# A decoder block on Trainium2: layer-norm scalings of a closed pair taken together, and gates turned at another place

## The chip, the cores and the metric

One core of a Trainium2 chip runs the whole kernel in one launch. The metric is the device time in microseconds. The core has five engines with queues of their own: TensorE (PE in the profile, its weight loads PEld), VectorE (DVE), ScalarE (ACT), GpSimd (POOL) and SyncE (SP), which issues all the DMA transfers named here.

## The reference, cut to what matters

`x` is (16, 256, 512) in float32. Three layers follow each other, each with its own residual and layer norm: a state-space mixer, a long convolution with multiplicative heads, and a feed-forward layer with two of eight low-rank experts for each token.

```python
# second layer (v = x, both factors = ctx), eight heads to a group
kv = vr[:, :, :, None, :] * x2r[:, :, None, :, :]
y = irfft(rfft(kv, n=1024) * k_f[None, :, None, None, :], n=1024)[..., :512]
y = y + kv * skip
out = einsum('bhijl,bhil->bhjl', y, x1r)
...
# third layer
base = x_flat @ W.T + b
logits = x_flat @ gate_w.T + gate_b
topk_logits, topk_idx = top_k(logits, 2)
gates = softmax(topk_logits)
xA = einsum('nd,erd->ner', x_flat, lora_A)
out = base + sum over the two chosen experts of gate * (xA @ lora_B)
...
x = layernorm(x + mixer(x))
x = layernorm(x + long_convolution(x))
x = layernorm(x + feed_forward(x))
```

## The kernel before

The first half of the kernel (up to about 750 us) is the mixer; the change doesn't touch it. The second half is one Python loop over 32 heads (`for h in range(HX)`). The order in which instructions are written is the order in each engine's queue: the kernel asks for a manual schedule, so that nothing is reordered, and only the waits are derived.

A head is a tile of 128 tokens' rows by 512. In iteration `h` the kernel does the long convolution of head `h` and, beside it, the feed-forward layer of head `f = h - 1`.

The convolution is a product with blocks of a Toeplitz matrix. It runs twice in each head, for the halves `q = 0` and `q = 1` of the batch, and accumulates in the four PSUM banks of `y`. Each half begins with `seeded` (L1013), a matmul into the last bank; ScalarE then copies parts of it into another bank (`spread_seed`, L1020); then `convolve` runs the full blocks (L1031) and the triangular ones in quadrants (L1046). In the midst of the quadrants TensorE waits for a tiny ScalarE copy, `one` (L1062), which itself waits for the first quadrants. When a half is done, VectorE multiplies the two pairs of banks by the context (`multiplied`, L1079, tile `pr`) and sums them (`reduced`, L1089, tile `red`). `y` has one buffer for each pair of banks, so the next seed can only be written when the first of the two products has read its bank. VectorE also makes the next head's `kv` (L157, `products`).

At the start of an iteration TensorE transposes the next head's `v` (`turned_v`, L147, copied by ScalarE at L149). Then come matmuls of the feed-forward layer as filling, then the seed.

The feed-forward layer of head `f` goes in these steps. GpSimd adds `ol` (L1412), ScalarE squares it (L1191), GpSimd folds the squares (L1195). `products_with_gates`, behind the first convolution, transposes the folded squares (L1211), multiplies `ol` by the gates' and low-rank weights (L1213) into the PSUM tile `gl`, and also transposes the gated low-rank products `xa` of the head before (L1209) into free columns of the new `gl` (`XAT`, the last 128); ScalarE copies that to `xaT` (L1225). `spread_of` makes the layer norm's factor `rs_h` on GpSimd (L1235). `gates` is a chain of small VectorE operations with one exponential on ScalarE (L1128 to L1147), ending in `xa`.

The dense product is done for two heads together with seven half products instead of eight (`class Pair`): `first`, `second`, `third_and_fifth`, `fourth`, `sixth`, `seventh` (all L1271) into the PSUM tiles `al` and `be`, and the low-rank additions `lora_of_first` and `lora_of_second`. Sums of inputs (`S`, L1289) are made on GpSimd. A pair that starts with `f` odd takes `f` and `f + 1`; from the next even `h` it is `closing`. `common` makes the shared sums `u` and `m` on VectorE; `scaled_first` and `scaled_others` make scaled copies `ua`, `ub`, `mb` on GpSimd (L1328, L1329). Head 0 of the feed-forward layer goes alone (`base`, `alone`).

The last layer norm of a head is `finish`: two VectorE scalings with running sums into `x3` (L1161), a negative mean on GpSimd (`nm_c`, L1103), a square with a sum on ScalarE (L1112), and three small GpSimd operations (L1114, L1115, L1166). `store` is one ScalarE activation (`res`, L1171) and a DMA. Before the change, head 0 of a closing pair is finished behind the second convolution of an even `h` and stored at the start of the next iteration behind the seed; head 1 is finished in the first half of that odd `h` and stored in its second half.

The order in the odd iteration, before the change:

```python
                if ready is not None:
                    store(*ready)
...
                elif closing is not None:
                    ready = closing.finish(1, folded)
```

and at the end of the even one:

```python
                convolve(y, kv, T, Td, 1)
                if closing is not None:
                    ready = closing.finish(0, closing.scaled_others)
```

Behind the loop, the last head's second convolution runs with `late=True`: quadrants first, then six full blocks, with the remaining steps of the last pair put between them (`steps`: `second`, `turn`, `lora_of_first`, `first_finished`, `rest`). The last head's own feed-forward layer and three stores follow.

Of the kernel before, what the change touches and what calls it, by code (L numbers as in the profile page):

```python
# [8 lines left out]
F32 = mybir.dt.float32  # L9
AF = mybir.ActivationFunctionType  # L10
# [62 lines left out]
def decoder_kernel(  # L73
# [843 lines left out]
    with ExitStack() as s2:  # L917
# [180 lines left out]

        def centred_squares(src, total, tag, between=None):

            nm = p2.tile([P, 1], F32, tag=f"nm_{tag}", name=f"nm_{tag}")
            if total.shape[1] == 2:
                nc.gpsimd.tensor_scalar(  # L1103
                    nm, total[:, 0:1], total[:, 1:2], -1.0 / D, ALU.add, ALU.mult
                )
            else:
                nc.gpsimd.tensor_scalar(nm, total, -1.0 / D, None, ALU.mult)
            if between is not None:
                between()
            sq = p2.tile([P, D], F32, tag="sq", name="sq")  # L1110
            var = p2.tile([P, 1], F32, tag=f"var_{tag}", name=f"var_{tag}")
            nc.scalar.activation(sq, src, AF.Square, bias=nm, accum_out=var)  # L1112
            rs = p2.tile([P, 1], F32, tag=f"rs_{tag}", name=f"rs_{tag}")
            nc.gpsimd.tensor_scalar(var, var, 1.0 / D, LN_EPS, ALU.mult, ALU.add)  # L1114
            nc.gpsimd.tensor_tensor(rs, var, nhalf[:, 0:1], ALU.pow)  # L1115
            return nm, rs

        def gates(gl, rs, room=None):
# [37 lines left out]

        def finish(h, parts, rs, between=None):
            x3 = p2.tile([P, D], F32, tag="x3", name="x3")
            total = p2.tile([P, len(parts)], F32, tag=f"sum_c{len(parts)}", name="sum_c")
            for n, (cols, ps, own) in enumerate(parts):  # L1160
                nc.vector.scalar_tensor_tensor(  # L1161
                    x3[:, cols], ps, rs, own, ALU.mult, ALU.add, accum_out=total[:, n : n + 1]
                )
            nm, rs = centred_squares(x3, total, "c", between)
            nb = p2.tile([P, 1], F32, tag="nb", name="nb")
            nc.gpsimd.tensor_tensor(nb, nm, rs, ALU.mult)  # L1166
            return h, x3, nb, rs

        def store(h, x3, nb, rs):
            res = p2.tile([P, D], F32, tag="res", name="res")  # L1170
            nc.scalar.activation(res, x3, AF.Identity, bias=nb, scale=rs)  # L1171
            nc.sync.dma_start(out[h * P : (h + 1) * P, :], res)

# [30 lines left out]

        def products_with_gates(o_l, sq, xa):

            gl = ps_t.tile([P, D], F32, tag="tr", name="gl")
            if xa is not None:
                nc.tensor.transpose(gl[0:ER, XAT], xa.rearrange("p e r -> p (e r)"), ident)  # L1209
            turned = gl[:, NG + 2 : NG + 2 + P]  # L1210
            nc.tensor.transpose(turned, sq, ident)  # L1211
            for kc in range(KD):
                nc.tensor.matmul(  # L1213
                    gl[:, 0 : NG + 2], o_l[:, kc, :], w_gl[:, kc, :],
                    start=(kc == 0), stop=(kc == KD - 1), skip_group_check=True,
                )
            ms = p2.tile([P, 1], F32, tag="ms", name="ms")
            nc.scalar.activation(
                sq, turned, AF.Identity, bias=eps, scale=1.0 / D, accum_out=ms
            )  # L1220
            return gl, ms

        def turned_copy(room):
            xaT = p2.tile([ER, P], F32, tag="xaT", name="xaT")
            nc.scalar.copy(xaT, room[0:ER, 0:P])  # L1225
            return xaT

        def spread_of(gl, ms):
# [9 lines left out]
        def turned_gates(xa, room):  # L1238
            nc.tensor.transpose(room[0:ER, 0:P], xa.rearrange("p e r -> p (e r)"), ident)
            return turned_copy(room)  # L1240

# [34 lines left out]
        class Pair:  # L1276
# [86 lines left out]

            def finish(self, head, between=None):
                return finish(self.f + head, self.parts(head), self.rs[head], between)

        last, xa = None, None
        pair, closing, ready = None, None, None
        for h in range(HX):
# [9 lines left out]
            if h:  # L1379
                if nxt:  # L1380
                    v_after = turned_v(vns.pop(0), ps_t, "tr")
                    kvs.append(load_T(h + 1))
                    if h + 2 < HX:
                        vns.append(load_v(h + 2))
                        cTs.append(load_c(h + 2))
                opened = pair if pair is not None and len(pair.o) == 2 else None
                if h == 2:
                    feed_forward(base, alone, (1,))
                if h == 3:
                    lora(base, xaT, ALL)  # L1390
                if opened is not None:
                    opened.sixth()
                if closing is not None:
                    closing.seventh()
                seed = seeded(y, T, xs, 0, h == 1)
                spread_seed(y, seed, h == 1)
                if ready is not None:
                    store(*ready)
                    ready = None
                if h == 2:  # L1400
                    feed_forward(base, alone, (2,))
                if opened is not None:
                    opened.second()
                if closing is not None:
                    closing.lora_of_second()
            if h < 2:
                weight_differences((3, 1) if h == 0 else (2, 4))
            if ff:
                for i, pr in zip(order, prs):
                    reduced(pr, red_f, 1, i)  # L1410
                o_l = p2.tile([P, NL, P], F32, tag="ol", name="ol", bufs=3)
                nc.gpsimd.tensor_tensor(  # L1412
# [5 lines left out]
                sq, folded = squares(o_l)  # L1418
                if h == 3:
                    ready = finish(0, ((ALL, base, b_bc),), rs_alone, folded)  # L1420
                elif closing is not None:
                    ready = closing.finish(1, folded)
                    closing = None
                else:
                    folded()
                if pair is not None and len(pair.o) == 2:
# [8 lines left out]
            red = p2.tile([P, NQ, NL, BQ * NH], F32, tag="red", name="red")  # L1435
            convolve(y, kv, T, Td, 0, late=h == 0, ahead=None if h else ahead)
            if h == 0:
                v_after = vT_ahead[0]
# [20 lines left out]
            if ff:  # L1459
                gl, ms = products_with_gates(o_l, sq, xa)  # L1460
                if xa is not None:
                    xaT = turned_copy(gl[:, XAT])
                    for one in (pair, closing):
                        if one is not None and one.f <= f - 1 <= one.f + 1:
                            one.xaT.append(xaT)
                if second:
                    pair.first()
                if closing is not None:
                    closing.fourth()
                    closing.scaled_first()  # L1470
                rs = spread_of(gl, ms)
                if second and nxt:
                    pair.sums_second()
            if nxt:
                seed = seeded(y, T, xs, 1, h == 0)
            if ff:
# [14 lines left out]
                if closing is not None:  # L1491
                    closing.lora_of_first()
            if ready is not None:
                store(*ready)
                ready = None
            if nxt:
                spread_seed(y, seed, h == 0)
            if nxt:
                products(v_n, cT_n, kv_n, 1)
# [5 lines left out]
            if ff:  # L1505
                if second and nxt:
                    pair.sums_third()
                if not nxt:
                    pair.common()
                xa = gates(gl, rs, gl[:, NG + 2 :])  # L1510
            if nxt:
                convolve(y, kv, T, Td, 1)
                if closing is not None:
                    ready = closing.finish(0, closing.scaled_others)
            else:
                pair.scaled_first()
                pair.scaled_others()
# [4 lines left out]
        o_f, red_f, y_f, cT_f = last  # L1522
        gl_f, o_l = gl, {}

# [45 lines left out]

        def turn():
            pair.xaT.append(turned_gates(xa, gl_f[:, XAT]))
            pair.fourth()
# [5 lines left out]
        def first_finished():  # L1579
            ready.append(pair.finish(0))  # L1580

# [20 lines left out]
        nc.tensor.matmul(base, xaT, w_lb, start=False, stop=True, skip_group_check=True)  # L1602
        store(*ready[0])
        store(*pair.finish(1))
        x3 = p2.tile([P, D], F32, tag="x3", name="x3")
# [80 lines left out]
```

## Time and profile before

| what | value |
|---|---|
| median of 3 runs | 1414.12 us (1413.99 to 1414.58) |
| the profiled execution | 1413.62 us, span 1411.80 us |
| TensorE busy | 1396.9 us, 99% of the span, 7091 matmuls |
| VectorE busy | 1178.7 us, 83% |
| GpSimd busy | 612.9 us, 43% |
| ScalarE busy | 429.2 us, 30% |
| granted TensorE clock | 0.998 |
| VectorE waiting for the convolution (L1079 on L1046) | 56.5 us in 46 waits |

A profile is one execution. In a timeline line the columns are the start in us, the length in us, the engine, the line of the kernel, the operation, output and inputs, and shapes; `x4` says that four such instructions are merged, and brackets give the idle time of the engine ahead of it and what ended that. Ends of matmuls are modelled, so for TensorE the distance from one start to the next says more than a length.

### The profile page before, as it was taken

The numbers are of one execution on the slowest core, as the hardware profiler recorded it, in microseconds if no ns is written. First come the engines' busy times: TensorE is split into PE (matmuls) and PEld (weight loads), VectorE is DVE, ScalarE is ACT, GpSimd is POOL, SyncE is SP. The second block draws the span as 40 slices with busy tenths as digits, with TensorE's granted clock in tenths as the row PEclk, the third lists the DMA queues.
The fourth block names the chain that finished last, engine by engine and source line by source line (L and its number), as shares of the span: only waits on it lengthen the run. The fifth ranks groups of instructions, "written<-read, shape, count | busy, mean of one in ns | idle before, by whom it ended". The sixth has DMA issues, their size and how long they took to land.

```text
span 1411.8 us, 19609 instructions
## 1 busy us (share of the span) xinstructions
PE 1396.9 (99%) x7091; PEld 949.5 (67%) x7091; DVE 1178.7 (83%) x2269; ACT 429.2 (30%) x948; POOL 612.9 (43%) x818
## 2 busy tenths in 40 slices
PE   9999999999999999999999999999999999999997
PEld 7888888788888888878885445454545554555444
DVE  6988878878888787877857888888989888989886
ACT  2423323233232332332311223333323233333331
POOL 5450011110100201001005577788777777887774
PEclk9999999999999999999999999999999999999999
DMA  8113111120121111202103112221222122212200
GB/s 304 33 38 133 36 57 46 38 84 8 46 77 46 52 40 39 85 18 81 47 8 116 50 48 75 76 68 53 75 68 68 45 75 75 75 47 74 68 25 32
DMA packets 49170, 89.22 MB, mean 63 GB/s; under 512 B 8880, under 2 KB 13360, under 8 KB 49072
## 3 DMA queue, kind: packets, MB, share of 16 engines
q1 hardware_dynamic: 49072, 87.96, 19.1%
q8 instruction: 56, 0.92, 0.3%
q14 instruction: 42, 0.34, 0.1%
HBM read 70.62 MB, written 17.32 MB: 62 GB/s over the span
## 4 chain that ended last, share of the span: by engine, by line
PE 95%; DVE 2%; issue 1%; DMA 1%; POOL 0%; ACT 0%; SPq 0%; POOLq 0%; DVEq 0%; ACTq 0%
PE mm L330 21%; PE y L1031 15%; PE s L330 14%; PE y L1046 12%; PE s L782 6%; PE mm L782 6%; PE y L1013 4%; PE be L1271 4%; PE al L1271 3%; PE gl L1213 2%; PE tr L147 1%; PE xm L599 1%; PE mm L739 1%; PE mm L873 1%; PE al L1243 1%; PE s L873 1%
## 5 line engine op out<-in xcount | busy, mean ns | idle before, releaser
L1079 DVE TENSOR_TENSOR pr<-y,cT 128x1024 f32<-128x1024 f32 x126 | 148.3, 1219 | 56.5 <-PE y L1046 56.5
L1046 PE MATMUL y<-kv 64*64 64x512 f32 x1536 | 179.8, 598 | 1.5 <-ACT one L1062 1.5
L588 DVE SCALAR_TENSOR_TENSOR acc<-xi,wc,acc 128x512 f32<-128x512 f32 x192 | 141.9, 753 | 7.4 <-ACT acc L584 1.7
L1089 DVE TENSOR_REDUCE red<-pr 128x128 f32<-128x1024 f32 x126 | 147.1, 1209 | 0.0
L157 DVE TENSOR_TENSOR kv<-tr,cT 128x1024 f32<-128x1024 f32 x124 | 145.4, 1214 | 0.0
L1046 PEld LDWEIGHTS y<-kv 64*64 64x64 f32 x1536 | 52.2, 132 | 120.3 <-issue 96.4
L1031 PE MATMUL y<-kv 128*128 128x512 f32 x272 | 128.5, 594 | 1.9 <-DVE pr L1079 1.7
L68 POOL TENSOR_TENSOR rs_a<-ve_a,nhalf 128x1 f32<-128x1 f32 x32 | 18.9, 592 | 242.7 <-DVE ve_a L66 242.7
L391 POOL TENSOR_TENSOR rstd<-ms,nhalf 128x4 f32<-128x4 f32 (+1 forms) x9 | 8.5, 949 | 251.6 <-DVE ms L389 251.6
L1031 PE MATMUL y<-kv,Td 128*128 128x512 f32 x248 | 116.6, 592 | 0.0
L330 PE MATMUL mm<-XT,w_z 128*128 128x256 f32 x384 | 90.7, 379 | 0.0
L1031 PEld LDWEIGHTS y<-kv,Td 128*128 128x128 f32 x248 | 47.2, 190 | 59.2 <-issue 55.6
L1020 ACT COPY y<-y 64x512 f32<-64x512 f32 x120 | 67.0, 558 | 45.4 <-PE y L1013 43.1
L997 POOL TENSOR_TENSOR xs<-kv 128x512 f32<-128x512 f32 x63 | 80.2, 1273 | 0.1
L1031 PEld LDWEIGHTS y<-kv 128*128 128x128 f32 x272 | 51.1, 190 | 42.7 <-ACT y L1020 17.9
L330 PEld LDWEIGHTS mm<-XT,w_z 128*128 128x128 f32 x384 | 73.1, 190 | 9.7
L330 PE MATMUL mm<-xnT,w_z 128*128 128x256 f32 x288 | 70.8, 382 | 0.0
L1412 POOL TENSOR_TENSOR ol<-o,red 128x512 f32<-128x512 f32 x31 | 39.3, 1269 | 68.3 <-DVE red L1089 68.3
L223 POOL TENSOR_TENSOR XT<-xnT 128x512 f32<-128x512 f32 x7 | 9.3, 1335 | 129.0 <-PE mm L782 123.7
L1013 PE MATMUL y<-xs,kv 128*128 128x512 f32 x120 | 63.8, 613 | 0.6
L330 PE MATMUL s<-XT,w_xi 128*128 128x256 f32 x256 | 61.0, 380 | 0.7 <-DVE XT L226 0.5
L330 PEld LDWEIGHTS mm<-xnT,w_z 128*128 128x128 f32 x288 | 54.1, 190 | 10.0 <-issue 3.0
(335 smaller groups left out, 3058.0 us busy)
## 6 DMA issues: line engine op xcount, KB each, us to landing
cT<-in_ctxT SPq DMA_DIRECT2D x32, 384.0 KB
kv<-in_toep SPq DMA_DIRECT2D x32, 384.0 KB
xt<-in_x SPq DMA_DIRECT2D x32, 256.0 KB
spread<-both SPq DMA_DIRECT2D x32, 256.0 KB
first<-xt SPq DMA_DIRECT2D x32, 256.0 KB
vn<-first SPq DMA_DIRECT2D x32, 256.0 KB
out<-res SPq DMA_DIRECT2D x31, 256.0 KB
xnT<-in_xT SPq DMA_DIRECT2D x7, 1024.0 KB
```

Source lines behind the costliest of these rows:

```text
L157: last = nc.vector.tensor_tensor(kv[:, q, k * BQ : (k + NL // 2) * BQ], vT[:, q, blks].rearrange("p k (b i) -> p (k b) i", i=NH).unsqueeze ...
L330: nc.tensor.matmul(ps, w[:, p, a, kc, :], Xs[b][:, kc, :], start=start and kc == 0, stop=stop and kc == 1, skip_group_check=upon,)
L588: ins = nc.vector.scalar_tensor_tensor(acc, xi[:, :, k : k + S], wc[:, c, k : k + 1], acc, ALU.mult, ALU.add)
L782: nc.tensor.matmul(ps, own[a][c][:, n * P : (n + 1) * P], w_o[b][c], start=start and c == 0, stop=stop and c == HC - 1, skip_group_check=upon,
L997: return nc.gpsimd.tensor_tensor(xs[:, q], moving(kv, q, 0), moving(kv, q, 1), ALU.add)
L1013: nc.tensor.matmul(seed, T[:, SHARED_AT, :], xs[:, q], start=True, stop=True)
L1020: nc.scalar.copy(bank_of(y, 2)[b : b + HP], seed[a : a + HP])
L1031: nc.tensor.matmul(bank_of(y, lb), w, moving(kv, q, mb), start=not late and lb not in begun, stop=False, skip_group_check=True,)
L1046: return nc.tensor.matmul(bank_of(y, lb)[cols], T[rows, DIAGONAL_AT, (b - a) * HP : (b - a + 1) * HP], moving(kv, q, lb)[rows], start=star ...
L1079: nc.vector.tensor_tensor(pr.rearrange("p (k b j) i -> p k b j i", k=2, j=NH), y[i].rearrange("p k (b j i) -> p k b j i", j=NH, i=NH), cT[ ...
L1089: nc.vector.tensor_reduce(red[:, q, 2 * i : 2 * i + 2, :].rearrange("p k t -> p (k t)"), pr, AX.X, ALU.add)
L1271: nc.tensor.matmul(ps, a[:, kc, :], w[:, kc, :], start=(start and kc == 0), stop=(kc == 1), skip_group_check=True,)
```

## The change

It has four parts.

- `finish` and `store` become a class `Finish`, so that its steps can be placed one by one: the constructor has the two VectorE scalings, then `mean`, `squares`, `spread`, and `store`; `whole` does the three in the middle at once.
- Both heads of a closed pair are scaled together in the first half of the odd iteration, behind the last sums (`reduced`) of the convolution of the head before. The means of both follow `ol` on GpSimd; the square and the factors of head 0 stand around the folding; those of head 1 behind the first convolution. Both are stored behind the second seed's copies. `scaled_others` moves ahead of the second convolution of the even iteration.
- The transpose of `xa` leaves `products_with_gates`. It now stands at the start of the next iteration, behind the transposes of `v`, and goes into the old `gl`.
- The gates of the pair's last head leave the loop and are made in `turn`, inside the last convolution; so ScalarE's exponential stands behind `one` in its queue. `pair.common` moves to the same branch as the last `scaled_first` and `scaled_others`.

The operations and their shapes stay the same; places change, and each GpSimd mean of a single sum reads one column of a two-column tile.

```diff
-        def finish(h, parts, rs, between=None):
...
+        class Finish:
+            def __init__(self, h, parts, rs):
...
+                for n, (cols, ps, own) in enumerate(parts):
+                    nc.vector.scalar_tensor_tensor(
+                        self.x3[:, cols], ps, rs, own, ALU.mult, ALU.add,
+                        accum_out=self.total[:, n : n + 1],
+                    )
...
-        def products_with_gates(o_l, sq, xa):
+        def products_with_gates(o_l, sq):
             gl = ps_t.tile([P, D], F32, tag="tr", name="gl")
-            if xa is not None:
-                nc.tensor.transpose(gl[0:ER, XAT], xa.rearrange("p e r -> p (e r)"), ident)
...
+                if xa is not None:
+                    xaT = turned_gates(xa, gl[:, XAT])
+                    if h == 2:
+                        xaT_alone = xaT
+                    else:
+                        pair.xaT.append(xaT)
...
                 spread_seed(y, seed, h == 1)
-                if ready is not None:
-                    store(*ready)
-                    ready = None
...
                 for i, pr in zip(order, prs):
                     reduced(pr, red_f, 1, i)
+                ready = []
+                if h == 3:
+                    ready = [Finish(0, ((ALL, base, b_bc),), rs_alone)]
+                elif closing is not None:
+                    ready = [closing.finish(head) for head in range(2)]
+                    closing = None
...
                 sq, folded = squares(o_l)
-                if h == 3:
-                    ready = finish(0, ((ALL, base, b_bc),), rs_alone, folded)
-                elif closing is not None:
-                    ready = closing.finish(1, folded)
-                    closing = None
-                else:
-                    folded()
+                for one in ready:
+                    one.mean()
+                for one in ready[:1]:
+                    one.squares()
+                folded()
+                for one in ready[:1]:
+                    one.spread()
...
             convolve(y, kv, T, Td, 0, late=h == 0, ahead=None if h else ahead)
+            for one in ready[1:]:
+                one.squares()
+                one.spread()
...
-                gl, ms = products_with_gates(o_l, sq, xa)
-                if xa is not None:
-                    xaT = turned_copy(gl[:, XAT])
...
+                gl, ms = products_with_gates(o_l, sq)
...
-            if ready is not None:
-                store(*ready)
-                ready = None
             if nxt:
                 spread_seed(y, seed, h == 0)
+            for one in ready:
+                one.store()
...
-                if not nxt:
-                    pair.common()
-                xa = gates(gl, rs, gl[:, NG + 2 :])
+                if closing is not None:
+                    closing.scaled_others()
+                if nxt:
+                    xa = gates(gl, rs, gl[:, NG + 2 :])
             if nxt:
                 convolve(y, kv, T, Td, 1)
-                if closing is not None:
-                    ready = closing.finish(0, closing.scaled_others)
             else:
+                pair.common()
                 pair.scaled_first()
                 pair.scaled_others()
...
         def turn():
+            xa = gates(gl_f, rs_f, gl_f[:, NG + 2 :])
             pair.xaT.append(turned_gates(xa, gl_f[:, XAT]))
...
-        store(*ready[0])
-        store(*pair.finish(1))
+        ready[0].store()
+        pair.finish(1).whole().store()
```

More of the change, by code (lines that the diff above doesn't have):

```diff
@@ L1097, in contract @@
                 reduced(pr, red, q, i)
[L1099 to L1105, printed above, removed]
-            else:
[L1107 to L1116, printed above, removed]
         def gates(gl, rs, room=None):
@@ L1155, in gates @@
             return xa
-        def finish(h, parts, rs, between=None):
[L1158 to L1172, printed above, removed]
+        class Finish:
+            def __init__(self, h, parts, rs):
+                self.h = h
+                self.x3 = p2.tile([P, D], F32, tag="x3", name="x3")
+                self.total = p2.tile([P, 2], F32, tag="sum_c", name="sum_c")
+                self.n = len(parts)
+                for n, (cols, ps, own) in enumerate(parts):
[3 more added lines that the diff above has]
+                    )
+            def mean(self):
+                self.nm = p2.tile([P, 1], F32, tag="nm_c", name="nm_c")
+                total = self.total
+                if self.n == 2:
+                    nc.gpsimd.tensor_scalar(
+                        self.nm, total[:, 0:1], total[:, 1:2], -1.0 / D, ALU.add, ALU.mult
+                    )
+                else:
+                    nc.gpsimd.tensor_scalar(self.nm, total[:, 0:1], -1.0 / D, None, ALU.mult)
+            def squares(self):
+                sq = p2.tile([P, D], F32, tag="sq", name="sq")
+                self.var = p2.tile([P, 1], F32, tag="var_c", name="var_c")
+                nc.scalar.activation(sq, self.x3, AF.Square, bias=self.nm, accum_out=self.var)
+            def spread(self):
+                var = self.var
+                self.rs = p2.tile([P, 1], F32, tag="rs_c", name="rs_c")
+                nc.gpsimd.tensor_scalar(var, var, 1.0 / D, LN_EPS, ALU.mult, ALU.add)
+                nc.gpsimd.tensor_tensor(self.rs, var, nhalf[:, 0:1], ALU.pow)
+                self.nb = p2.tile([P, 1], F32, tag="nb", name="nb")
+                nc.gpsimd.tensor_tensor(self.nb, self.nm, self.rs, ALU.mult)
+            def whole(self):
+                self.mean()
+                self.squares()
+                self.spread()
+                return self
+            def store(self):
+                res = p2.tile([P, D], F32, tag="res", name="res")
+                nc.scalar.activation(res, self.x3, AF.Identity, bias=self.nb, scale=self.rs)
+                nc.sync.dma_start(out[self.h * P : (self.h + 1) * P, :], res)
@@ L1221, in products_with_gates @@
             return gl, ms
[L1223 to L1226, printed above, removed]
         def spread_of(gl, ms):
@@ L1239, in turned_gates @@
             nc.tensor.transpose(room[0:ER, 0:P], xa.rearrange("p e r -> p (e r)"), ident)
-            return turned_copy(room)
+            xaT = p2.tile([ER, P], F32, tag="xaT", name="xaT")
+            nc.scalar.copy(xaT, room[0:ER, 0:P])
+            return xaT
         def lora(ps, xaT, cols, start=False):
@@ L1362, in parts, with finish @@
                 return (LO, self.be[:, HI], self.own[2]), (HI, self.al[:, HI], self.own[3])
-            def finish(self, head, between=None):
-                return finish(self.f + head, self.parts(head), self.rs[head], between)
+            def finish(self, head):
+                return Finish(self.f + head, self.parts(head), self.rs[head])
         last, xa = None, None
-        pair, closing, ready = None, None, None
+        pair, closing, ready = None, None, []
         for h in range(HX):
@@ L1385, in decoder_kernel @@
                         cTs.append(load_c(h + 2))
+                if xa is not None:
+                    xaT = turned_gates(xa, gl[:, XAT])
+                    if h == 2:
+                        xaT_alone = xaT
+                    else:
+                        pair.xaT.append(xaT)
                 opened = pair if pair is not None and len(pair.o) == 2 else None
@@ L1389, in decoder_kernel @@
                 if h == 3:
-                    lora(base, xaT, ALL)
+                    lora(base, xaT_alone, ALL)
                 if opened is not None:
@@ L1418, in decoder_kernel @@
                 sq, folded = squares(o_l)
-                if h == 3:
-                    ready = finish(0, ((ALL, base, b_bc),), rs_alone, folded)
-                elif closing is not None:
-                    ready = closing.finish(1, folded)
-                    closing = None
-                else:
-                    folded()
+                for one in ready:
[5 more added lines that the diff above has]
+                    one.spread()
                 if pair is not None and len(pair.o) == 2:
@@ L1459, in decoder_kernel @@
             if ff:
-                gl, ms = products_with_gates(o_l, sq, xa)
-                if xa is not None:
-                    xaT = turned_copy(gl[:, XAT])
-                    for one in (pair, closing):
-                        if one is not None and one.f <= f - 1 <= one.f + 1:
-                            one.xaT.append(xaT)
+                gl, ms = products_with_gates(o_l, sq)
                 if second:
@@ L1522, in decoder_kernel @@
         o_f, red_f, y_f, cT_f = last
-        gl_f, o_l = gl, {}
+        gl_f, rs_f, o_l = gl, rs, {}
         def contracted(src, ks):
@@ L1579, in first_finished @@
         def first_finished():
-            ready.append(pair.finish(0))
+            ready.append(pair.finish(0).whole())
         def rest():
```

## The prediction

> **What bounds the kernel now.** I read the page first (busy shares, then the chain), then the stretch 1082.14 to 1122.24 us, which is one pair of heads in the steady part, then the timeline of TensorE at the joints of these heads, and last the timeline of the end.
>
> ```profile
> PE 95%; DVE 2%; issue 1%; DMA 1%; POOL 0%; ACT 0%; SPq 0%; POOLq 0%; DVEq 0%; ACTq 0%
> ...
> 1082.14:1122.24 40.10, 40.07 (x202) 20.25 (x201) 35.86 (x62) 12.91 (x32) 31.68 (x43) 1.00 0.20 66
> ```
>
> The first line is the chain that ended last: 95% of it is TensorE. The second is the pair: length, then busy time of PE, PEld, DVE, ACT, POOL. PE has no hole, DVE is idle 4.2 us of 40.1, POOL 8.4 us. A busy share doesn't show small stalls of PE, so I take spacings of starts. I call T the end of a head's second convolution (its first v transpose starts there) and J the end of its first one.
>
> ```profile
> 1088.24 0.66 PE L147 MATMUL tr<-ident,vn 128*128 128x128 f32 x4
> 1088.73 1.03 PE L1271 MATMUL be<-Tw,ol 128*128 128x256 f32 x4
> 1089.79 1.10 PE L1013 MATMUL y<-xs,kv 128*128 128x512 f32 x2
> ...
> 1097.85 0.33 PE L1209 MATMUL gl<-ident,xa 128*128 128x128 f32 x1
> 1098.02 0.27 PE L1211 MATMUL gl<-ident,sq 128*128 128x128 f32 x1
> 1098.13 1.11 PE L1213 MATMUL gl<-w_gl,ol 128*128 128x138 f32 x8
> ...
> 1108.79 0.66 PE L147 MATMUL tr<-ident,vn 128*128 128x128 f32 x4
> 1109.28 1.03 PE L1271 MATMUL al<-Tw,S 128*128 128x256 f32 x4
> 1110.21 0.67 PE L1013 MATMUL y<-xs,kv 128*128 128x512 f32 x1
> ```
>
> The first group is T of an odd head (h = 17), the second its J, the third T of the even head after it. From T to the seed (L1013) an odd head takes 1.55 us, an even one 1.42. Four v transposes take 0.49 of it; four 256-column matmuls need 4 x 0.215 (1099.08 to 1099.94, where nothing waits) = 0.86. So PE is ready for the seed at T + 1.35 and waits in both. For what, VectorE's timeline shows:
>
> ```profile
> 1088.07 0.48 DVE L1161 SCALAR_TENSOR_TENSOR x<-be,rs_h,ua 128x256 f32<-128x256 f32 x1
> 1088.47 2.35 DVE L1079 TENSOR_TENSOR pr<-y,cT 128x1024 f32<-128x1024 f32 x2
> ...
> 1097.96 2.36 DVE L1079 TENSOR_TENSOR pr<-y,cT 128x1024 f32<-128x1024 f32 x2 [1.22 <-PE y L1046]
> ...
> 1108.89 2.35 DVE L1079 TENSOR_TENSOR pr<-y,cT 128x1024 f32<-128x1024 f32 x2 [1.46 <-PE y L1046]
> ```
>
> The seed writes the bank that the first of the two products reads. In the even head that product starts at T + 0.10, in the odd one at T + 0.23, behind the two scalings of head 0 of the closed pair. The first product takes 1.2 us, and the seed follows it by 0.1. So TensorE bounds the kernel, but at each T it waits for VectorE a little. Behind such a wait the seed's second pass also starts late: 0.50 us after the first, against 0.43 at J, so the wait is really 0.075 longer than its start shows (seed in effect at T + 1.495 in even heads).
>
> [...]
>
> **The change, part by part.**
> *Gates' transpose out of J.* L1209 goes; L1211 becomes the first behind the convolution and inherits its 0.17, so one 0.11 is saved (1098.02 to 1098.13). The seed of J is not held by VectorE: it stands at J + 2.09, and the product that it needs ends at about J + 1.3. The saving holds in h = 3 to 30: 28 x 0.11 = 3.1 us. In h = 2 little stands ahead of the seed and it waits for VectorE anyway (nothing); h = 31 belongs to the end below.
> *The same transpose into T.* PE is then ready at 1.35 + 0.11 = T + 1.46, the seed could run in effect at 1.495 anyway: cost nothing in even heads; if that cover is gone, 0.11 each. It reads `xa`, finished at 1087.75 ahead of T = 1088.24, in even heads 1.3 us ahead; it is at its turn at T + 0.49. Queued behind it on PE are `seventh` or `sixth` and the seed, so a late `xa` would now cost at once; 0.9 us are in hand. The copy (0.26 us on ACT) goes behind the copy of v, T + 1.3 to 1.6, ahead of the seed's copies, which can't start before T + 2.5: hidden.
> *Scalings of head 0 out of T of odd heads.* The product starts at T + 0.10 instead of 0.23: 0.13 each. The seed comes at the even heads' time, which PE's own 1.46 just allows. Odd heads 5 to 29: 13 x 0.13 = 1.7 us. Bounds per head: 0.04 (PE arrives late by a weight load) and 0.165 (the slow second pass goes too).
> *The same scalings behind the sums.* Two more of 0.40 us on DVE in the first half of the odd head. It had 1.22 us idle ahead of J; it gains 0.13 by starting sooner, gives 0.80, and J comes 0.13 sooner: 0.42 us are left. Cost nothing; without that cover each 0.1 us short costs 1.4 us in all.
> *POOL.* `ub` and `mb` (1088.89 to 1092.35, four operations, 3.4 us) move ahead of the even head's last convolution, into the 4.3 us that POOL idles before the next `ol` plus what they leave. In the odd head `ol` starts at T + 4.85 (as in even ones) instead of 5.26; then two means, folding, variance, power, product (1.05 together) and the sums S as before, and then the same 1.05 for the second head, ahead of `t`: `t` at about T + 11.7 instead of 11.05, so rs_h at 15.25 instead of 14.6. DVE needs rs_h at 16.64 (1104.88). The second pair sum `xs` ended at 1108.67, 0.12 ahead of the next T; now 0.65 later against a T that comes 0.24 sooner: T + 0.8, and the seed is issued at T + 1.39. Cost nothing, some 0.5 us in hand.
> *ACT.* The square of head 0 leaves the front of the copy of v; in the odd head it ends at about T + 7.5, and the small copy that TensorE's quadrants wait for (L1062) is due at T + 7.9. The second square stands behind that copy. The store's two activations (0.81 each) now stand behind the seed's copies of J instead of ahead (1100.41 ahead of 1101.25). Cost nothing.
> *SP.* Two `out` transfers are issued together at about T + 14.5; behind them stand the next head's three loads, issued at the next T (20.4). Nothing.
> *The end.* Three lines:
>
> ```profile
> 1385.04 0.55 POOL L1235 TENSOR_TENSOR rs_h<-var_b,nhalf 128x1 f32<-128x1 f32 x1
> ...
> 1386.78 1.09 PE L1046 MATMUL y<-kv 64*64 64x512 f32 x8 [1.49 <-ACT one L1062]
> ...
> 1389.63 0.27 PE L1239 MATMUL gl<-ident,xa 128*128 128x128 f32 x1
> ```
>
> PE waits 1.49 us for L1062, which stands on ACT behind the exponential of the last gates, which wait for rs_h behind POOL's `o`. The change takes this wait away: PE reaches the gates' transpose about 1.5 us sooner, but `xa` isn't there. It ended at 1388.19; with POOL's extra 1.05, less 0.4 for the earlier `ol`, at 0.65 later. From there DVE (sums, product and reduction, scalings) leads to `seventh`, which must wait for the scalings some 0.6 us. Before, PE's end was 9.65 us behind the start of `xa`, after it 8.85: 0.8 gained, 0.65 to 0.7 given back, 0.1 left. Bounds: minus 0.5 and plus 0.7.
>
> Sum: 3.1 + 1.7 + 0.1 = 4.9 us. The profiled execution took 1413.62 us (span 1411.80 and 1.82 around it), so 1408.7 on its scale; the median of the three runs is 0.5 higher, so 1414.12 - 4.9 = 1409.2.
>
> **Rivals.**
> *Everything at its better bound*: also the slow second passes vanish (13 x 0.035 in odd, 13 x 0.035 in even heads) and the end brings 0.7: 6.4 us, 1407.7. For it: PE's readiness and VectorE's differ by 0.03 us only. Against: they differ on VectorE's side.
> *The transpose is only moved*: at T it costs its 0.11 after all, since it delays a weight load behind which the seed is issued. Then 3.1 is given back and 1.7 + 0.1 stay: 1412.3, no change that can be told. For it: the margin is 0.03. Against: in both kinds of head PE waits at T today.
> *POOL becomes late* (slower): the second head's variance chain stands ahead of `t` in the odd head, and everything behind it, `xs` among it, moves. If the seed at the next T waits for the whole of `xs`, and POOL runs more than 0.5 us later than counted, each further us costs PE 1 us in 14 odd heads; it turns the sign from 0.85 us beyond my count (0.35 x 14 = 4.9). At 1.2 us it gives 1414.1 - 4.9 + 9.8 = 1419. For it: POOL waits in order for DVE's scalings before it can fold. Against: it idles 4.28 us per pair.
>
> **How the numbers follow.** Forecast 0.60, better bound 0.12, moved only 0.14, POOL late 0.14. A change under 0.2% (2.8 us) can't be told from none. Faster 0.73, same 0.14, slower 0.13. The range takes in the better bound and the moved-only case and leaves most of the slower one out: 1406.8 to 1413.2.
>
> **What would show it.** Right: the pair at 39.75 us instead of 40.10; T to seed 1.42 to 1.46 in both kinds of head; J to seed 1.98; DVE's first product at T + 0.10 in odd heads and 0.3 to 0.5 us of idle ahead of J there; no wait of L1046 for L1062 at the end, but one of the gates' transpose for `xa`. Wrong: PE waiting at T for `xs` or `xa`, a product at J without idle time before it, or the seed at T + 1.5 and more.

## The result

| | median | runs | ratio to before, 95% interval |
|---|---|---|---|
| before | 1414.15 us | 6 (1413.30 to 1414.58) | |
| changed | 1408.63 us | 6 (1408.25 to 1409.31) | 0.9961 [0.9949, 0.9974] |
| before, measured again | 1413.71 us | 13 (1413.08 to 1414.82) | |
| changed, measured again beside it | 1408.96 us | 5 (1408.80 to 1409.42) | 0.9967 [0.9955, 0.9980] |

The change makes the kernel 5.5 us faster in the first comparison and 4.75 in the second; 4.9 was forecast. The profiled execution has a span of 1406.6 us, against 1411.8. The page's chain and the stretch of one pair (the same two heads as shown of before; length, then PE, PEld, DVE, ACT and POOL busy):

```profile
PE 96%; DVE 2%; issue 1%; DMA 0%; POOL 0%; ACT 0%; SPq 0%; POOLq 0%; DVEq 0%
```

```profile
1066.23:1105.99 39.76, 39.76 (x204) 20.21 (x200) 35.97 (x61) 12.76 (x31) 31.71 (x43) 1.00 0.21 66
```

A pair takes 39.76 us instead of 40.10. TensorE still sets the time; VectorE's work is the same in a shorter pair, so it has 3.8 us of idle time instead of 4.2. The seed is one matmul and stands in these lists as two instructions (`L1013 ... x2`), which the prediction calls passes. TensorE's timeline shows T of an odd head, its J, and T of the even head behind it:

```profile
1085.68 0.66 PE L147 MATMUL tr<-ident,vn 128*128 128x128 f32 x4
1086.18 0.27 PE L1244 MATMUL gl<-ident,xa 128*128 128x128 f32 x1
1086.29 1.03 PE L1278 MATMUL be<-Tw,ol 128*128 128x256 f32 x4
1087.15 1.06 PE L1013 MATMUL y<-xs,kv 128*128 128x512 f32 x2
1088.05 0.59 PE L1360 MATMUL be<-w_lb,xaT 128*128 128x256 f32 x2
...
1095.17 0.33 PE L1221 MATMUL gl<-ident,sq 128*128 128x128 f32 x1
1095.34 1.11 PE L1223 MATMUL gl<-w_gl,ol 128*128 128x138 f32 x8
...
1097.15 1.02 PE L1013 MATMUL y<-xs,kv 128*128 128x512 f32 x2
...
1105.99 0.66 PE L147 MATMUL tr<-ident,vn 128*128 128x128 f32 x4
...
1107.46 1.06 PE L1013 MATMUL y<-xs,kv 128*128 128x512 f32 x2
```

From T to the seed (L1013) it is now 1.47 us in both kinds of head (before 1.55 and 1.42), with the gates' transpose (L1244) between; from J to the seed 1.98 (before 2.09).

The start of the seed alone misleads here: by it even heads lose 0.05 at each T and odd ones gain only 0.08. Where the seed waits at T its second pass is late too (0.505 us behind the first in the kernel before and 0.466 now, against 0.43 at J in both), so the distance to count is from T to the first matmul behind both passes. In the odd head (T is 1088.24) of the kernel before, that matmul is

```profile
1090.73 0.60 PE L1353 MATMUL be<-w_lb,xaT 128*128 128x256 f32 x2
```

which is T + 2.49; now it is the line at 1088.05, T + 2.37. Over the 13 odd heads from 5 to 29 and the 13 even ones from 6 to 30 the medians are:

| T to the matmul behind the seed | odd heads | even heads |
|---|---|---|
| before | 2.485 us | 2.364 us |
| changed | 2.363 us | 2.363 us |

Odd heads gain 0.12 us, and even heads take in the 0.11 us of the transpose and lose nothing. VectorE's timeline at the same two places of the odd head:

```profile
1085.79 2.35 DVE L1079 TENSOR_TENSOR pr<-y,cT 128x1024 f32<-128x1024 f32 x2 [0.48 <-PE y L1046]
...
1095.28 2.36 DVE L1079 TENSOR_TENSOR pr<-y,cT 128x1024 f32<-128x1024 f32 x2 [0.40 <-PE y L1046]
```

At T the product starts 0.11 behind the transposes and VectorE was idle for 0.48 us before it; at J 0.40 us are left of 1.22.

To see where the time went I cut the spans at two marks that all kernels have: the first T of the pairwise steady work (`h` = 1) and the last J (`h` = 31). What lies ahead of the first mark holds nothing of the change, and over the traces of this case it differs by up to 1.2 us (770.13 to 771.30).

| | to T of h = 1 | T of h = 1 to J of h = 31 | J of h = 31 to the end |
|---|---|---|---|
| before | 770.56 | 608.01 | 33.23 |
| changed | 770.28 | 603.21 | 33.10 |
| changed, once more | 771.30 | 603.21 | 33.11 |

The loop gains 4.80 us and the end 0.13; the rest of the 5.2 us between the two spans is that first stretch.

### The profile page after: what moved, and what is told of

Same layout as the page of the kernel before. It is cut to its first block, busy times and chain, and to the rows that moved or that the text cites. A ratio compares the mean times of both kernels' runs of the same rounds, so it can differ in the third digit from the quotient of the medians.

```text
span 1406.6 us, 19577 instructions
## 1 busy us (share of the span) xinstructions
PE 1391.9 (99%) x7091; PEld 946.6 (67%) x7091; DVE 1182.1 (84%) x2269; ACT 427.5 (30%) x948; POOL 613.3 (44%) x818
## 4 chain that ended last, share of the span: by engine, by line
PE 96%; DVE 2%; issue 1%; DMA 0%; POOL 0%; ACT 0%; SPq 0%; POOLq 0%; DVEq 0%
PE mm L330 21%; PE y L1031 15%; PE s L330 14%; PE y L1046 12%; PE s L782 6%; PE mm L782 6%; PE y L1013 4%; PE be L1278 4%; PE al L1278 3%; PE gl L1223 2%; PE tr L147 1%; PE xm L599 1%; PE mm L739 1%; PE mm L873 1%; PE al L1250 1%; PE s L873 1%
## 5 line engine op out<-in xcount | busy, mean ns | idle before, releaser
L1013 PE MATMUL y<-xs,kv 128*128 128x512 f32 x120 | 62.6, 604 | 0.5 <-issue 0.2
```

Of the source, the lines that this page charges most:

```text
L1013: nc.tensor.matmul(seed, T[:, SHARED_AT, :], xs[:, q], start=True, stop=True)
```

## The experiments

**One part at a time.** The first two kernels split the change in the loop. In one the gates' transpose goes back to J:

```diff
-                if xa is not None:
-                    xaT = turned_gates(xa, gl[:, XAT])
...
+        def products_with_gates(o_l, sq, xa):
             gl = ps_t.tile([P, D], F32, tag="tr", name="gl")
+            if xa is not None:
+                nc.tensor.transpose(gl[0:ER, XAT], xa.rearrange("p e r -> p (e r)"), ident)
```

> The changed kernel with the gates' transpose and its copy put back behind the first convolution (J); all else as changed. My theory (the transpose saves 0.11 us at each J of h = 3 to 30 and costs nothing at T; the scalings save 0.13 us at each T of the odd heads, apart from it): J to the seed back at 2.08, T to the seed 1.42 to 1.43 in both kinds of head, a pair about 39.97 us, the whole 2.5 to 3.1 us slower than the changed kernel, about 2 us faster than the kernel before. Rival (the two parts share one gain, since both shorten the way to the seed at T): less than 1 us of the gain is lost.

Measured: 1411.83 us, 0.9987 [0.9980, 0.9993] of before. T to the seed is 1.43 in both kinds of head, J to the seed 2.08; the loop takes 606.29 us, 3.08 more than in the changed kernel, which is 28 x 0.11. T of an odd head and its seed:

```profile
1087.50 0.66 PE L147 MATMUL tr<-ident,vn 128*128 128x128 f32 x4
...
1088.93 1.10 PE L1013 MATMUL y<-xs,kv 128*128 128x512 f32 x2
```

From T to the matmul behind the seed it is 2.363 us here too (median, odd and even heads), with no transpose between. So the transpose costs nothing at T in the changed kernel, and the scalings with the moves that go with them gain 1.72 us alone, which is 13 x 0.13; the rival falls.

In the other the transpose alone is moved, in the kernel before:

```diff
+                if xa is not None:
+                    xaT = turned_gates(xa, gl[:, XAT])
...
-        def products_with_gates(o_l, sq, xa):
+        def products_with_gates(o_l, sq):
             gl = ps_t.tile([P, D], F32, tag="tr", name="gl")
-            if xa is not None:
-                nc.tensor.transpose(gl[0:ER, XAT], xa.rearrange("p e r -> p (e r)"), ident)
```

> The kernel before with the transpose alone moved to T. My theory: J to the seed 1.97, T to the seed unchanged at 1.55 in odd heads and 1.43 to 1.47 in even ones, a pair about 39.88 us, the whole 2.7 to 3.1 us faster than before. Rival (the transpose only changes its place and costs its 0.11 at T again): within 0.5 us of before, T to the seed 1.66 and 1.54.

Measured: 1412.21 us, 0.9989 [0.9983, 0.9996]; the loop takes 606.57 us, a gain of 1.44, half of what I expected. J to the seed is 1.97 as foreseen, but T to the seed is 1.67 in odd heads:

```profile
1087.35 0.66 PE L147 MATMUL tr<-ident,vn 128*128 128x128 f32 x4
...
1089.02 1.10 PE L1013 MATMUL y<-xs,kv 128*128 128x512 f32 x2
```

Neither of the two theories says this: to the matmul behind the seed it is 2.363 us in even heads, which lose nothing, and 2.601 in odd ones, which lose 0.12. VectorE's timeline of this kernel, from the product at J of an even head to the one at T of the odd head:

```profile
1077.49 2.36 DVE L1079 TENSOR_TENSOR pr<-y,cT 128x1024 f32<-128x1024 f32 x2 [0.79 <-PE y L1046]
...
1086.89 0.48 DVE L1161 SCALAR_TENSOR_TENSOR x<-al,rs_h,b_bc 128x256 f32<-128x256 f32 x1
1087.29 0.48 DVE L1161 SCALAR_TENSOR_TENSOR x<-be,rs_h,ua 128x256 f32<-128x256 f32 x1
...
1087.69 2.35 DVE L1079 TENSOR_TENSOR pr<-y,cT 128x1024 f32<-128x1024 f32 x2
```

The last line has no bracket: VectorE came to it without waiting for another engine. From one product to the other it needs 10.20 us here, and 10.19 in the kernel before, from this line to the product at 1088.47 that the prediction shows:

```profile
1078.28 2.36 DVE L1079 TENSOR_TENSOR pr<-y,cT 128x1024 f32<-128x1024 f32 x2 [0.79 <-PE y L1046]
```

With the scalings in this stretch, VectorE and not TensorE sets it, and 0.11 saved on TensorE at J is waited for at T. The two parts of the change need each other: 1.44 and 1.72 alone, 4.80 together.

**Is it VectorE's work in that stretch?** I took one small operation out of it, in the kernel with the transpose alone moved. The gates of these heads then leave out the tie-breaking that the layer needs; the kernel serves to time this stretch and for nothing else.

```diff
-            nc.vector.tensor_tensor(cmp[:, :, 1, :], cmp[:, :, 1, :], tri, ALU.mult)
+            if ties:
+                nc.vector.tensor_tensor(cmp[:, :, 1, :], cmp[:, :, 1, :], tri, ALU.mult)
...
-                xa = gates(gl, rs, gl[:, NG + 2 :])
+                xa = gates(gl, rs, gl[:, NG + 2 :], closing is None)
```

> The kernel before with the transpose alone moved, and in the even heads from h = 4 on the gates leave out one VectorE operation (the multiplication that breaks ties, 0.23 us, some 0.26 with its spacing). My theory now (from an even head's J to the odd head's T VectorE has no idle time in the kernel before, so what TensorE saves at that J is lost again at T): the first product of odd heads starts at T + 0.10, T to the seed falls from 1.67 to 1.47, and the whole is 2.4 to 3.0 us faster than with the transpose alone moved. Rival (the transpose itself costs its 0.11 at the T of odd heads): T to the seed stays at 1.67 and the time stays.

Measured: 1408.93 us, 3.3 less than with the transpose alone; the loop takes 603.49 us instead of 606.57, 3.08 less. The seed of the odd head (T, the transposes, and the seed in TensorE's timeline; then VectorE's product):

```profile
1086.08 0.66 PE L147 MATMUL tr<-ident,vn 128*128 128x128 f32 x4
1086.57 0.27 PE L1238 MATMUL gl<-ident,xa 128*128 128x128 f32 x1
1086.68 1.03 PE L1270 MATMUL be<-Tw,ol 128*128 128x256 f32 x4
1087.55 1.06 PE L1013 MATMUL y<-xs,kv 128*128 128x512 f32 x2
```

```profile
1086.18 2.36 DVE L1079 TENSOR_TENSOR pr<-y,cT 128x1024 f32<-128x1024 f32 x2
```

is back at T + 1.47 with the transpose still ahead of it, and the product at T + 0.10. That holds in 12 of the 13 odd heads; in `h` = 27 VectorE lost 0.23 us among the gates' operations in this execution, for a reason that the profile doesn't show, and the seed came at T + 1.70. So two different reliefs of VectorE's queue in the second half of even heads, this one and the change itself, bring the same T + 1.47: that queue is shown to be the cause, and the transpose at T costs nothing by itself.

**GpSimd's cover.** The slower rival of the prediction was a late second `xs`. Two additions on constants stand ahead of `t`:

```diff
             for one in ready[1:]:
                 one.squares()
                 one.spread()
+                if nxt:
+                    for _ in range(2):
+                        more = p2.tile([P, HD], F32, tag="more", name="more", bufs=1)
+                        nc.gpsimd.tensor_tensor(more, b_bc[:, LO], b_bc[:, HI], ALU.add)
```

> The changed kernel with two idle GpSimd additions (128 x 256, 0.73 us each, 1.6 with spacing, on constants) behind the second head's variance chain in odd heads. They move t, rs_h and the second xs 1.6 us later; the second xs then ends at about T + 2.5 of the even head. Theory of the slower rival (the seed waits for the whole of xs): T to the seed 2.5 in even heads, 13 to 15 us slower than the changed kernel. Other theory (the seed waits only for its own half of xs): no wait of TensorE, less than 0.5 us slower.

Measured: 1409.36 us (1408.64 to 1409.79). The median lies 0.4 to 0.7 us above those of the changed kernel, but in the profiled execution the loop takes 603.22 us, within 0.01 of that kernel's. GpSimd's second `xs`, and the seed of the even head on TensorE (T is 1106.54):

```profile
1107.70 1.29 POOL L997 TENSOR_TENSOR xs<-kv 128x512 f32<-128x512 f32 x1
```

```profile
1108.01 1.06 PE L1013 MATMUL y<-xs,kv 128*128 128x512 f32 x2
```

The seed starts 0.98 us ahead of the end of that operation: it waits for its own half of `xs` only. So the slower rival, which had the seed wait for the whole of `xs`, is refuted.

**VectorE's cover in the odd head.** The same with VectorE, behind the four scalings, two and four times (`n` stands for 2 and 4):

```diff
                     ready = [closing.finish(head) for head in range(2)]
                     closing = None
+                    for _ in range(n if nxt else 0):
+                        more = p2.tile([P, HD], F32, tag="more", name="more", bufs=1)
+                        nc.vector.tensor_tensor(more, b_bc[:, LO], b_bc[:, HI], ALU.add)
```

> The changed kernel with two idle VectorE additions (128 x 256, about 0.4 us each, on constants) behind the four scalings in odd heads, against 0.40 us of idle time ahead of J. As the prediction prices it (each 0.1 us short costs 1.4 us): 4 to 6 us slower than the changed kernel. Other theory (the seed of J comes 1.97 us behind J and its product needs 1.3, so another 0.35 to 0.4 us are covered): less than 1 us slower.

> The changed kernel with four such VectorE additions. As the prediction prices it: 1.1 to 1.2 us short, 15 to 17 us slower than the changed kernel. Other theory (cover of 0.75 to 0.8 us in all): J to the seed 2.7 in odd heads, 9 to 11 us slower.

Measured: 1409.00 us with two and 1425.33 us with four (1.0081 [1.0067, 1.0095] of before). With two the product at J comes 0.31 us later than without and the loop takes 603.21 us: nothing is lost. With four, VectorE's added group, its product, and TensorE from J (1103.50) to the seed:

```profile
1100.25 2.35 DVE L1429 TENSOR_TENSOR more<-b_bc 128x256 f32<-128x256 f32 x4
...
1105.39 2.34 DVE L1079 TENSOR_TENSOR pr<-y,cT 128x1024 f32<-128x1024 f32 x2
```

```profile
1103.50 0.33 PE L1221 MATMUL gl<-ident,sq 128*128 128x128 f32 x1
...
1106.65 1.12 PE L1013 MATMUL y<-xs,kv 128*128 128x512 f32 x2 [1.01 <-DVE pr L1079]
```

The product is 1.78 us late (J + 1.89 instead of 0.11) and the seed 1.18 (J + 3.15 instead of 1.97). So 0.60 us are covered behind the idle 0.40. The four took 2.3 us (1100.25 to the next operation at 1102.53) and not 1.6, which is why the cost passed my figure of 9 to 11: the half takes 12.10 us instead of 10.82, and 13 x 1.28 = 16.6 us, which the loop shows (619.80). The two of the kernel with two took 0.80 us (1092.51 to 1093.31); what lengthened the four isn't shown. That these 16.6 us fall into the 15 to 17 of the prediction's price is luck: the work was 0.7 us longer than priced, and the cover 0.6 us larger.

**The end.** In the next kernel the last gates are made in the loop again:

```diff
-                if nxt:
-                    xa = gates(gl, rs, gl[:, NG + 2 :])
+                if not nxt:
+                    pair.common()
+                xa = gates(gl, rs, gl[:, NG + 2 :])
...
-            xa = gates(gl_f, rs_f, gl_f[:, NG + 2 :])
```

> The changed kernel with the last head's gates made in the loop again, ahead of the last convolution. My theory (the change of the end gains 0.8 us on the way from the last gates to TensorE's end, and GpSimd's second variance chain ahead of rs_h gives 0.65 to 0.7 of it back): the quadrants wait about 2.1 us for L1062, and the whole is 0.6 to 1.0 us slower than the changed kernel. Rival (nothing is gained there, since xa is what TensorE waits for in both): the same within 0.2 us.

Measured: 1411.12 us, and widely spread (1409.27 to 1412.58): 2.2 to 2.5 us slower than the changed kernel, where I expected 0.6 to 1.0. In its profile the end takes 37.17 us, 4.07 more than in the changed kernel. TensorE's wait (2.51 us) is near the 2.1 that I expected, but what follows is slow (TensorE's timeline; then windows, where the figure behind the busy times is the granted clock):

```profile
1382.46 1.99 PE L1046 MATMUL y<-kv 64*64 64x512 f32 x8 [2.51 <-ACT one L1062]
1384.38 2.07 PE L1278 MATMUL al<-w_f,ol 128*128 128x256 f32 x4
```

```profile
1380.00:1382.00 2.00, 0.00 (x0) 0.00 (x0) 0.63 (x4) 0.00 (x0) 1.92 (x3) 1.00 0.00 0
1382.00:1384.00 2.00, 1.54 (x8) 0.30 (x8) 1.72 (x10) 0.38 (x2) 1.83 (x4) 0.51 0.00 0
1384.00:1388.00 4.00, 4.00 (x11) 2.13 (x8) 0.95 (x3) 0.00 (x0) 2.38 (x3) 0.50 0.00 0
```

The four matmuls of the second line take 1.13 us in the changed kernel. The granted clock fell from 1.00 to 0.50 in the wait and came back behind 1388 (0.56 from 1388 to 1389, then 1.00). In the 21 runs the seven fastest (up to 1410.19 us) all had a mean granted clock of 0.998; of the 14 from 1410.88 us on, 11 had 0.997 or 0.996. To part the two causes I filled the wait:

```diff
             for e in QUADRANTS[4:8]:
                 quadrant(*e)
+            for _ in range(3 if steps else 0):
+                nc.tensor.matmul(y[1][:, 0, :], T[:, 0, :], moving(kv, q, 0), start=True, stop=True)
```

> The last gates in the loop again, and three idle matmuls of 512 columns into an unused bank, written between the quadrants that TensorE has done and those that wait for L1062 in the last convolution (2.6 us of work in a wait of 2.6 us). Theory (the wait of 2.5 us let the granted clock fall to a half, and that made the end 4.1 us longer instead of 0.8): the clock stays at 1.00, the end from the last J takes 33.7 to 34.3 us, 0.6 to 1.2 us slower than the changed kernel. Rival (the order of the end costs 4 us whatever the clock is): 36 to 37.5 us from the last J.

Measured: 1410.13 us (1409.58 to 1410.83), clock 1.00, end 34.28 us. That is what the theory said (33.7 to 34.3), and the rival falls. So in these profiles the order alone costs 1.2 us (34.28 against 33.10; the filling, 2.77 us from its start to the next quadrants, outlasts the wait of 2.51 by some 0.2), and the clock the other 2.9. The seven fastest runs without the filling give an estimate of the order's cost too: their median is 1409.71 us, 0.75 above the 1408.96 of the changed kernel.

The last kernel takes up what the prediction saw as given back: in the last head the second head's variance chain and the sum S4 (`sums_third`) stand behind rs_h on GpSimd.

```diff
                     if not nxt:
                         pair.sums_second()
-                        pair.sums_third()
...
             for one in ready[1:]:
                 one.squares()
-                one.spread()
+                if nxt:
+                    one.spread()
...
                 rs = spread_of(gl, ms)
+                if not nxt:
+                    pair.sums_third()
...
-            for one in ready:
+            for one in ready if nxt else ready[:1]:
                 one.store()
...
                 pair.scaled_first()
+                held = ready[1]
+                held.spread()
                 pair.scaled_others()
...
             pair.xaT.append(turned_gates(xa, gl_f[:, XAT]))
+            held.store()
```

> The changed kernel, and in the last head alone GpSimd's variance chain of the second head and the sum S4 stand behind rs_h, and that head's store behind the gates' transpose. My theory (rs_h behind GpSimd's queue decides the end): rs_h 1.7 us sooner, no wait of TensorE for xa, the whole 1.2 to 1.9 us faster than the changed kernel. Rival (VectorE's sums or TensorE's own work decide the end): less than 0.5 us.

Measured: 1407.06 us, 0.9954 [0.9941, 0.9966] of before. It was run once more, and the changed kernel beside it:

> The changed kernel itself, on the same chip as the two runs beside it: 5.0 to 5.6 us faster than before; from the last J to the end 33.1 us.

> The reordered end once more, beside the changed kernel: 1.5 to 1.9 us faster than it, 31.3 us from the last J to the end. Rival (the 1.6 us between the medians of different runs were drift of the chip): within 0.5 us of it.

Measured: 1407.04 us, 0.9954 [0.9940, 0.9968], against 1408.96 for the changed kernel (4.75 us faster than before, a little less than the 5.0 to 5.6 expected). The two differ by 1.9 us, and their runs don't overlap (1406.58 to 1407.84 against 1408.80 to 1409.42). The end takes 31.36 us instead of 33.11. Counted from the last J, rs_h starts at 5.41 us instead of 7.38 and `xa` at 8.30 instead of 10.18. The gates' transpose in the changed kernel, and then in this one:

```profile
1384.08 0.33 PE L1244 MATMUL gl<-ident,xa 128*128 128x128 f32 x1 [1.21 <-DVE xa L1128]
```

```profile
1382.86 0.27 PE L1244 MATMUL gl<-ident,xa 128*128 128x128 f32 x1
```

The wait for `xa` is gone. How much of it the variance chain brings and how much S4 isn't parted. This version beats both kernels.

## Why the prediction was right

- *What bounds the kernel.* TensorE, with small waits for VectorE at each T: right. The gain is the transpose put into the waits that are left, and the longer waits of odd heads brought down to those of even ones.
- *The sum.* 3.1 + 1.7 for the loop; the loop gained 4.80. 0.1 for the end; it gained 0.13. The medians differ by 5.5 and by 4.75; the stretch ahead of the loop, which the change doesn't touch, varies by more than that difference between profiled executions, but it wasn't measured for each run.
- *J.* 1.97 to 1.98 to the seed, as forecast, in every head from 3 to 30. The sum rests on the spacing of 0.11 us from the start of a transpose to the next start (1098.02 to 1098.13 before), not on its length in the trace, 0.27.
- *T.* Forecast 1.42 to 1.46, measured 1.47 in both kinds. To the matmul behind the seed odd heads gain 0.12 us and even ones nothing, as the parts "0.13 each" and "cost nothing in even heads" say; the scalings alone confirm the first (1.72 us). The rival that the transpose is only moved falls with the 2.363 us that stand with it and without it. Of the slow second passes about half went, 0.505 to 0.466 us, in both kinds of head; what they bring is spent by the seed's later start.
- *The sum's terms taken as separate: here it failed.* I gave 3.1 us to the transpose and 1.7 to the scalings as if each stood alone. The transpose alone brings 1.44. From J of an even head to T of the odd one VectorE worked for 10.19 us without waiting for another engine, and TensorE's saving at that J is real only because the scalings leave the same stretch. The sum came out right since both were made together; the account for each alone was not. The lines to see it were there: the odd head's product at T had no idle time in front of it.
- *VectorE's price.* "Each 0.1 us short costs 1.4 us in all" counted the idle 0.40 us as the whole cover. The seed of J adds 0.60: two additions made the product 0.31 us late and cost nothing.
- *GpSimd.* `t`, rs_h and the second `xs` came at T + 11.84, 15.38 and 0.90 (11.7, 15.25 and 0.8 forecast). That the seed might wait for the whole of `xs` is refuted.
- *The end.* The wait for L1062 went and one for `xa` came (1.21 us). From the start of `xa` to the end of the last convolution it is 8.64 us instead of 9.64, so 1.0 is gained where 0.8 was forecast; the wait filled with matmuls shows about the same (1.2, some 0.2 of it the filling). `xa` starts 0.91 us later behind the last J (10.18 instead of 9.27), where 0.65 to 0.70 was forecast. Both sizes were about 0.2 us small, and that they cancel is luck. Moving the chain and S4 gains 1.8 us. Unforeseen was the granted clock of 0.50 behind the longer wait there (2.51 us).

## What to carry to other kernels

When two queues are nearly in balance, find for each stretch between two meeting points which of them has no idle time; a saving on the other is worth nothing there until that one is lightened too (here 0.11 us saved and 0.12 waited for). Cover is counted to the next instruction that someone waits for, not to the end of the idle time (here 0.60 us more than the idle 0.40). And at the end of a kernel look at what stands in the queue ahead of the small operation that the last chain needs: it is cheap to let it go first (here 1.8 us at the end).

## What was not expected of the hardware

In the profiled execution of the kernel with the last gates in the loop the granted clock fell to 0.50 in TensorE's wait of 2.51 us and stayed at that for 6.8 us. That length is worked out from the mean clock of three stretches: 0.51 from 1382 to 1384, 0.50 from 1384 to 1388, 0.56 from 1388 to 1389. In the profiled executions with waits of 1.49 us (before) and 1.21 us (changed) the clock was 1.00 throughout these, and with the 2.51 us filled with matmuls it was 1.00 too.

It doesn't seem to happen in each execution of that kernel, since its times reach from 1409.27 to 1412.58 us and its mean granted clocks from 0.996 to 0.998. What decides it isn't shown: of that kernel there is the trace of one execution, and no run moves the wait or makes it shorter or longer by itself.
